# A twelve-layer decoder on one core: the logarithm of the state-space layer in parts between scans, and layer 2's causal mask added by TensorE

## The chip, the cores and the metric

One core of one Trainium2 chip runs the whole decoder in one launch. The metric is the device time of that launch in microseconds. The engines are named as in the profile: PE is TensorE (matmul; PEld are its weight loads), DVE is VectorE, ACT is ScalarE, POOL is GpSimd, SP is SyncE, which only issues DMAs here.

## The reference, cut to what matters

The input is four sequences of 512 tokens with 128 features, in fp32. Twelve sublayers run in turn, each followed by a residual sum and a layer normalization. Two of them are touched.

Layer 1's attention is a selective state-space layer: 256 inner channels with 16 states each.

```python
xc = silu(causal_conv(xi) + conv_b)
dt, Bm, Cm = split(xc @ W_x)
delta = softplus(dt @ W_dt + b_dt)
dA = exp(delta[..., None] * A);  dBu = delta[..., None] * Bm[:, :, None, :] * xc[..., None]
h = dA_t * h + dBu_t;  y = einsum('bdn,bn->bd', h, C_t)      # a scan over the 512 tokens
return (ys + xc * D) * silu(z) @ W_out
```

Layer 2's attention has 16 heads of width 64 and a causal mask.

```python
logits = jnp.einsum('bhik,bhjk->bhij', q, k)
logits = jnp.where(tril(ones((L, L))), logits, -1000000.0)
y = einsum('bhij,bhjv->bhiv', softmax(logits, axis=-1), kv)
```

## The kernel before

The order of instructions on every engine is the order in which the Python code issues them: the kernel switches the framework's own scheduling off, and the code interleaves by hand. A layer is a generator that issues a piece of work at each `yield`; heads and tails of neighbouring layers are interleaved, the bodies run alone. An `Agenda` maps a step number to pieces that are issued when `run(step)` is reached. The framework adds the semaphores that the data and the buffers need. Each engine takes its own queue in order, so a waiting instruction holds up all that stands behind it on its engine.

**The state-space layer** (`l1_attn`, from L1997) holds channels on partitions, in two halves c = 0 and 1 of 128, and time along the free axis. It goes through the four sequences; each has eight steps, and a step handles two of the 16 states. Below, "step 0" to "step 7" are the steps of one sequence (`j` in the code), and `g` counts them over all four. A step issues, in this order:
- `recurred(g)`: on DVE two products, du times the broadcast B (L2136, for c = 0 and 1), then two scans of 1024 elements (L2139); after each scan POOL multiplies the result h by C (L2143).
- `decays(g + 1)`: on ACT four exponentials da of the next step (L2125), two for each half of `de`.
- on PE `summed(g - 1, 0)` (L2152, adds h into the accumulator acc), then the pieces of the agenda `early`, then the broadcasts of B (pb, L2111) and C (pc, L2117) for the next step and half 0, then `summed(g - 1, 1)`, then pb and pc for half 1. ACT copies pc to cs (L2118).
- at step 0 the `outputs` of the sequence before: two DVE instructions on acc (L2161), a POOL product with the gate sz (L2164), and later a projection yps on PE (L2173, step 7), its sum with the residual (L2179), the statistics (L334, L335) and, at the next step 0, the normalization (L346) and the transposition.

While a sequence is scanned, the next one is prepared in pieces (`prepare`): the agenda `early` does the convolution of half 0 at step 1, of half 1 at step 2, `selected` (dt, B, C) at step 3, `exponentials(0)` at step 4 and `exponentials(1)` at step 5, and the gates (psz on PE, L2045, and Silu on ACT, L2046) at step 6. `exponentials(c)` makes on PE the tile pdt (L2065) and on ACT seven functions of it, three squares sq among them (L2076). The softplus needs a logarithm: `logarithm(c)` is a polynomial in five DVE instructions of 512 elements each (three at L2085, two at L2087), which work in place on the tile pdt. They are issued at the end of step 4 (half 0) and at the end of step 5 (half 1), after that step's scans. `ends` adds the result to `de` and makes `du` on POOL, two instructions of 1024 elements (L2090, L2091), at the head of step 6.

PSUM is tight here. pb tiles have two buffers, so the next step's pb of a half waits for this step's scan of that half. The tiles pscv, px, pdt, psz, yps and the transposes share a ring that has one bank, `a1`.

**Causal attention** (class `Causal`, L1112 to L1203) is used by layer 1's expert layer and by layer 2's attention (`l2_attn`, from L1453). A unit is a pair of heads of one sequence; layer 2 has 4 x 8 = 32 units. The query tiles of a unit are handled in three parts (`PARTS`): tile 3 with 512 keys; tiles 2 and 0 with 384 and 128; tile 1 with 256. For each part PE makes the scores of both heads (L1137), with one head in the upper and one in the lower 64 rows of the array. Then `maxima` on DVE does one `tensor_tensor_reduce` for each tile and head (L1153), eight in a unit: it adds the mask tile, negates, writes the result back to PSUM and reduces its minimum to nm. `exps` on ACT takes exp(-x + nm) and the sums zs (L1161), and `norm` divides on DVE (L1167) and POOL (L1170). `turned` transposes on PE (L1186), and `products` multiplies with v (L1199). The mask tile is bf16: 384 columns of zero and then 128 by 128 with -2^100 above the diagonal.

A step of layer 2 issues the scores of unit i + 1 and the rest of unit i; PE's order is: scores of part 0, the last product of the unit before, transposes of key part 0, queries and keys psqk of unit i + 2, scores of part 1, transposes, product 0, output projection ypo, scores of part 2, transposes psv of v, transposes, product 1. All these PSUM tiles take turns in a ring of three buffers, so each waits until the third one before it is read out. psv so waits for the exponentials of part 1.

Of the kernel before, what the change touches and what calls it, by code (L numbers as in the profile page):

```python
# [15 lines left out]
AF = mybir.ActivationFunctionType  # L16
ALU = mybir.AluOpType
AX = mybir.AxisListType
# [3 lines left out]
P = 128  # L22
B, S, D = 4, 512, 128
# [70 lines left out]
def _layer_params(name, p):  # L94
# [80 lines left out]
def decoder_kernel(ctx: ExitStack, tc: tile.TileContext, x, ctxT, mask1, mask3, packs, offsets, out, layers):  # L175
    nc = tc.nc
# [131 lines left out]
    identb = const.tile([P, P], BF16, name="identb")  # L308
# [803 lines left out]
    class Causal:  # L1112
# [4 lines left out]
        KEYS = (((0, 0),), ((1, 0), (3, 384)), ((2, 0),))  # L1117
        WIDTH = (512, 512, 256)

        def __init__(self, pool, room):  # L1120
            self.ap, self.room, self.work = pool, room, None

            self.mask = pool.tile([P, S], BF16, name="cmaskb", bufs=1)
            nc.gpsimd.memset(self.mask[:, : S - P], 0.0)
            make_causal_mask(nc, self.mask[:, S - P :], MASKED)
            self.nm = {}
            self.pr = {}
            self.pT = {}

        def scores(self, u, part, q, k):  # L1130

            sc = psum2("scc")
            for i, (qt, at) in enumerate(self.PARTS[part]):
                n = (qt + 1) * P
                for r in range(2):
                    rows = slice(64 * r, 64 * r + 64)
                    nc.tensor.matmul(  # L1137
                        sc[:, r, at : at + n], lhsT=q[rows, qt * P : n], rhs=k[rows, :n], start=(i == 0), stop=True,
                        skip_group_check=True,
                    )  # L1140
            nt = len(self.PARTS[part])
            nm = small.tile([P, 2, 2], F32, tag=f"nm{part}", name="nm")
            zs = small.tile([P, 2, 2], F32, tag=f"zs{part}", name="zs")
            pr = self.ap.tile([P, 2, self.WIDTH[part]], F32, tag=f"pr{part}", name="pr")
            self.pr[u, part] = pr

            def maxima():

                for i, (qt, at) in enumerate(self.PARTS[part]):
                    n = (qt + 1) * P  # L1150
                    for r in range(2):
                        of = sc[:, r, at : at + n]
                        nc.vector.tensor_tensor_reduce(  # L1153
                            of, of, self.mask[:, S - n :], -1.0, 3.0e38, ALU.add, ALU.min, nm[:, i, r : r + 1]
                        )

            def exps():
                for i, (qt, at) in enumerate(self.PARTS[part]):
                    to = at + (qt + 1) * P
                    for r in range(2):  # L1160
                        nc.scalar.activation(  # L1161
                            pr[:, r, at:to], sc[:, r, at:to], AF.Exp, bias=nm[:, i, r : r + 1], scale=-1.0,
                            accum_out=zs[:, i, r : r + 1],
                        )
# [40 lines left out]
    def l1_ffn(w, cur, new, last, room):  # L1205
        NH, NE, DH, NC = 8, 8, 64, 4
        units = B * NC
        keep, pool = room.take("keep"), room.take("early")
        causal = Causal(pool, room)
# [215 lines left out]
        first, then, last_of = gate(0)  # L1425
# [27 lines left out]
    def l2_attn(w, cur, new, last, room):  # L1453
        NC = 8
        units = B * NC
        keep, pool = room.take("keep"), room.take("early")
# [4 lines left out]
        causal = Causal(pool, room)  # L1461
        made, ypo, oTs = {}, {}, {}
        agenda = Agenda()
        state_x, state_T = cur["x"], cur["xT"]
# [532 lines left out]
    def l1_attn(w, cur, new, last, room):  # L1997
# [20 lines left out]

        das, work = [], []
        made = {}  # L2020
        early, late = Agenda(), Agenda()

        def prepare(b):

# [4 lines left out]
            ab = one.tile([P, 2, S], F32, tag="ab", name="ab")  # L2029
            ln = one.tile([P, 2, S], F32, tag="ln", name="ln")  # L2030
# [47 lines left out]
                    nc.scalar.activation(na, w["alog"], AF.Exp)  # L2078
                    nc.vector.tensor_scalar(na, na, -1.0, None, ALU.mult)

            def logarithm(c):

                e, sq = es.pop(c), squares.pop(c)
                for i, (_, _, number) in enumerate(LOG1P_T):
                    nc.vector.scalar_tensor_tensor(e, sq[:, i, :], number, e, ALU.add, ALU.mult)  # L2085
                for number, to in zip(LOG1P, (e, ln[:, c, :]), strict=True):
                    nc.vector.scalar_tensor_tensor(to, e, number, ab[:, c, :], ALU.add, ALU.mult)  # L2087
# [5 lines left out]
            return (  # L2093
                [
                    lambda: convolved(0), lambda: convolved(1), selected, lambda: exponentials(0),
                    lambda: exponentials(1), lambda: (gates(0), gates(1)),
                ],
                [lambda: logarithm(0), lambda: logarithm(1)],
                ends,
            )  # L2100

# [27 lines left out]
        def recurred(g):  # L2129

            b, j = divmod(g, steps)
            m = made[b]
            m["h", j] = [work[0].tile([P, NQ, S], F32, tag=f"hh{c}", name=f"hh{c}") for c in range(2)]
            pbs = [m.pop(("B", j, c)) for c in range(2)]
            for c in range(2):
                nc.vector.tensor_tensor(pbs[c], m["du"][:, c, None, :].to_broadcast([P, NQ, S]), pbs[c], ALU.mult)  # L2136
            for c in range(2):
                flat = m["h", j][c].rearrange("p n t -> p (n t)")
                nc.vector.tensor_tensor_scan(  # L2139
                    flat, das[g % 2][:, c].rearrange("p n t -> p (n t)"), pbs[c].rearrange("p n t -> p (n t)"),  # L2140
                    0.0, ALU.mult, ALU.add,
                )
# [51 lines left out]
        for i in (0, 1, 5, 2, 3, 4):  # L2194
            first[i]()
            yield PIECE
            if i in (3, 4):
                second[i - 3]()
# [15 lines left out]
        for g in range(total + 1):  # L2214
            b, j = divmod(g, steps)
            if j == 1 and b + 1 < B:
                first, second, third = prepare(b + 1)
                early.add(g, first)
                late.add(g + 3, second)
            if j == 6 and b + 1 < B:  # L2220
                third()
            if g < total:
                recurred(g)
            if g + 1 < total:
# [187 lines left out]
```

## Time and profile before

| what | value |
|---|---|
| runs | 2703.14 us median of 3 (2700.03 to 2704.36) |
| profiled execution | 2705.39 us; its span 2703.4 us, granted clock 0.963 |
| PE | 2410.7 us busy, 89% of the span |
| DVE | 1754.2 us, 65% |
| ACT | 1247.0 us, 46% |
| POOL | 1056.1 us, 39% |
| the state-space layer's steps | about 547 to 823 us |
| layer 2's causal attention | about 1437 to 1850 us |
| L2139, the 64 scans | 142.6 us, 2270 ns each |
| L1153, the 384 masked maxima (192 of them in the other layer) | 191.5 us, 499 ns each |
| L1137, scores | 142.5 us |

A profile line of a group names line, engine, operation, out<-in with partitions x elements and type, and a count; fp32 matmuls appear as two records each. A timeline line gives the start and the duration in us and merges neighbours of the same kind. In brackets stands the idle time of that engine just before, and the instruction whose end released it.

### The profile page before, as it was taken

The numbers are of one execution on the slowest core, as the hardware profiler recorded it, in microseconds if no ns is written. First come the engines' busy times: TensorE is split into PE (matmuls) and PEld (weight loads), VectorE is DVE, ScalarE is ACT, GpSimd is POOL, SyncE is SP. The second block draws the span as 40 slices with busy tenths as digits, with TensorE's granted clock in tenths as the row PEclk, the third lists the DMA queues.
The fourth block names the chain that finished last, engine by engine and source line by source line (L and its number), as shares of the span: only waits on it lengthen the run. The fifth ranks groups of instructions, "written<-read, shape, count | busy, mean of one in ns | idle before, by whom it ended". The sixth has DMA issues, their size and how long they took to land.

```text
span 2703.4 us, 37772 instructions
## 1 busy us (share of the span) xinstructions
PE 2410.7 (89%) x13974; PEld 1161.6 (43%) x13994; DVE 1754.2 (65%) x3484; ACT 1247.0 (46%) x2525; POOL 1056.1 (39%) x1376
## 2 busy tenths in 40 slices
PE   5898889978877989999999999997988999999998
PEld 1233334433334434444444555554455233446665
DVE  6796951288896665555556666666756887664444
ACT  3676432377652434333333455453543787443221
POOL 2342520166675336556542444443445343310000
PEclk9998999989998999999999999998998999999999
DMA  5421310000002400000000000002102241400000
GB/s 152 119 79 57 101 35 0 0 0 0 0 16 80 142 7 1 0 1 1 1 1 1 15 12 1 13 13 83 39 1 59 77 115 23 139 24 1 4 5 8
DMA packets 75560, 96.39 MB, mean 36 GB/s; under 512 B 23664, under 2 KB 62320, under 8 KB 75376
## 3 DMA queue, kind: packets, MB, share of 16 engines
q1 hardware_dynamic: 74224, 92.14, 11.7%
q8 instruction: 110, 1.80, 0.3%
q10 hardware_dynamic: 1152, 1.84, 0.2%
q14 instruction: 74, 0.61, 0.1%
HBM read 63.92 MB, written 33.49 MB: 36 GB/s over the span
## 4 chain that ended last, share of the span: by engine, by line
PE 62%; DVE 16%; ACT 9%; POOL 5%; issue 4%; DMA 2%; SPq 1%; POOLq 0%; DVEq 0%; ACTq 0%
PE psgu L1935 4%; PE psve L1289 4%; PE av L709 4%; PE yT L1332 3%; PE scc L1137 3%; PE ype L1946 3%; ACT pr L1161 3%; PE psh L1624 3%; DVE scc L1153 3%; PE avc L1199 3%; PE ptc L1186 3%; DVE top L967 2%; PE sc L670 2%; PE avx L995 2%; DVE top L674 2%
## 5 line engine op out<-in xcount | busy, mean ns | idle before, releaser
L1170 POOL TENSOR_TENSOR pr<-pr,zs 128x1024 f32<-128x1024 f32 x192 | 237.4, 1254 | 246.6 <-DVE zs L1167 232.4
L674 DVE TENSOR_REDUCE top<-sc 128x2 f32<-128x1024 f32 x256 | 300.8, 1216 | 46.8 <-PE sc L670 43.0
L695 ACT ACTIVATE pT<-st 128x512 f32<-128x512 f32 x512 | 276.1, 597 | 89.0 <-PE st L686 85.8
L1161 ACT ACTIVATE pr<-scc,nm 128x256 f32<-128x256 f32 (+3 forms) x384 | 199.0, 530 | 198.2 <-DVE zs L1167 78.3
L1153 DVE CUSTOM_DVE_ANT_0 scc<-scc,cmaskb 128x256 f32<-128x256 f32 (+3 forms) x384 | 191.5, 499 | 131.4 <-PE scc L1137 112.6
L967 DVE TENSOR_REDUCE top<-scx 128x4 f32<-128x616 f32 x256 | 192.1, 794 | 88.1 <-PE scx L954 77.2
L973 ACT ACTIVATE pTx<-stx 128x512 f32<-128x512 f32 x256 | 139.3, 596 | 202.8 <-PE scx L954 135.5
L2143 POOL TENSOR_TENSOR hh<-hh,cs 128x1024 f32<-128x1024 f32 x64 | 149.4, 2355 | 74.0 <-DVE hh L2139 50.1
L709 PE MATMUL av<-pT,vbuf 128*32 128x256 f32 x2048 | 162.8, 393 | 8.4 <-ACT avs L509 8.4
L492 POOL CAST nmP<-top 128x16 bf16<-128x16 f32 x96 | 25.6, 267 | 363.7 <-DVE top L967 202.5
L1294 DVE TENSOR_TENSOR vtmp<-psve,gm 128x1024 f32<-128x1024 f32 x64 | 78.3, 1224 | 133.2 <-PE psve L1289 133.1
L337 POOL TENSOR_TENSOR rsf<-mvf,eps 128x4 f32<-128x4 f32 x48 | 9.9, 206 | 393.7 <-DVE mvf L335 392.6
L1137 PE MATMUL scc<-k,q 64*128 64x512 f32 (+3 forms) x768 | 142.5, 469 | 10.8 <-ACT pr L1161 6.2
L1186 PE MATMUL ptc<-ident,pr 128*128 128x128 f32 x960 | 138.4, 282 | 10.3 <-ACT pT L1533 5.7
L2139 DVE TENSOR_TENSOR_SCAN hh<-da,pb 128x1024 f32<-128x1024 f32 x64 | 142.6, 2270 | 0.0
L1289 PE MATMUL psve<-w_L_ffn,xT 128*128 128x512 f32 x256 | 125.7, 615 | 17.4 <-ACT pr L1161 11.9
L670 PE MATMUL sc<-kP,qP 64*128 64x512 bf16 x512 | 106.3, 414 | 35.1 <-DMA qP<-far_q 16.6
L1299 POOL TENSOR_TENSOR vtmp<-vtmp 128x512 f32<-128x512 f32 x60 | 76.0, 1267 | 153.9 <-DVE vtmp L1294 133.6
L2152 PE MATMUL acc<-hh,ident 128*128 128x512 f32 x256 | 132.5, 644 | 3.1 <-DVE yt L2161 1.9
L1199 PE MATMUL avc<-pT,v 128*64 128x512 f32 (+3 forms) x768 | 131.2, 449 | 0.8 <-DVE pT L1522 0.5
L1186 PEld LDWEIGHTS ptc<-ident,pr 128*128 128x128 f32 x960 | 103.4, 141 | 55.1 <-issue 13.9
L1332 PE MATMUL yT<-gT,w_L_ffn 128*128 128x512 f32 x256 | 122.9, 603 | 0.0
(418 smaller groups left out, 5044.4 us busy)
## 6 DMA issues: line engine op xcount, KB each, us to landing
qP<-far_q SPq DMA_DIRECT2D x24, 768.0 KB, 6.3
w_L_ffn<-in_L_ffn SPq DMA_DIRECT2D x24, 512.0 KB, 6.5
far_q<-part SPq DMA_DIRECT2D x44, 192.0 KB, 2.8
qP<-far_q SPq DMA_DIRECT2D x24, 256.0 KB, 4.1
far_q<-part SPq DMA_DIRECT2D x44, 128.0 KB, 2.4
kP<-far_k SPq DMA_DIRECT2D x7, 768.0 KB, 5.3
kP<-far_kc SPq DMA_DIRECT2D x16, 231.0 KB, 4.5
w_L_attn<-in_L_attn SPq DMA_DIRECT2D x6, 512.0 KB, 6.6
```

The source lines that it names most:

```text
L674: return lambda: nc.vector.tensor_reduce(top[:, qt, 2 * gp : 2 * gp + 2], sc, AX.X, ALU.max, negate=True)
L695: nc.scalar.activation(pT, st, AF.Exp)
L709: nc.tensor.matmul(m["av"][32 * g : 32 * g + 32, part], lhsT=m["v"][:, kt, 4 * j + g, :], rhs=weights_of[s, g][:, part], start=(kt == 0 an ...
L967: nc.vector.tensor_reduce(ops.maxima(a)[:, 2 * qp : 2 * qp + 2, 2 * gp : 2 * gp + 2].rearrange("p i r -> p r i"), sc, AX.X, ALU.max, negat ...
L1137: nc.tensor.matmul(sc[:, r, at : at + n], lhsT=q[rows, qt * P : n], rhs=k[rows, :n], start=(i == 0), stop=True, skip_group_check=True,)
L1153: nc.vector.tensor_tensor_reduce(of, of, self.mask[:, S - n :], -1.0, 3.0e38, ALU.add, ALU.min, nm[:, i, r : r + 1])
L1161: nc.scalar.activation(pr[:, r, at:to], sc[:, r, at:to], AF.Exp, bias=nm[:, i, r : r + 1], scale=-1.0, accum_out=zs[:, i, r : r + 1],)
L1170: nc.gpsimd.tensor_tensor(pr[:, :, at : at + n], pr[:, :, at : at + n], zs[:, i, :, None].to_broadcast([P, 2, n]), ALU.mult)
L1186: nc.tensor.transpose(pt[:, r, to : to + P], self.pr[u, p][:, r, lo : lo + P], ident)
L1199: nc.tensor.matmul(av[64 * r : 64 * r + 64, kt * P :], lhsT=v[:, kt, 64 * r : 64 * r + 64], rhs=self.pT[u, part][:, r, at : at + n], start ...
L1289: nc.tensor.matmul(ps[:, r, :], lhsT=src[:, t * P : (t + 1) * P], rhs=w["ve"][:, h * 512 : (h + 1) * 512], start=True, stop=True,)
L1332: nc.tensor.matmul(yTs[b], lhsT=oe[:, c, e, :], rhs=gT[:, i, :], start=(c == 0 and e == 0), stop=(c == NC - 1 and e == NE - 1),)
```

## The change

In the state-space layer:
- The five instructions of each half's logarithm are split three and two. Half 0: three at the end of step 4 as before, two in step 5, between the two scans. Half 1: three between the scans of step 6, two between the scans of step 7.
- The sums `ends` work on one half at a time, with 512 elements: half 0 between the scans of step 6, half 1 between the scans of step 7, on POOL behind h of half 0.
- The gates move from step 6 to step 0 of the sequence itself.
- Before the first sequence the logarithms stay whole; the sums come in halves.

In layer 2's attention alone (`by_pe`):
- PE adds the mask: for each tile and head one more product, identity (bf16, weights) times the 128 by 128 mask, accumulated onto the last 128 columns of the scores; eight in a unit, 256 in all, each with its own weight load.
- DVE takes the negated maximum of the scores with one plain `tensor_reduce` for each tile and both heads, four in a unit, and doesn't write the scores back.
- The exponentials take scale 1 for -1.

```diff
-                        sc[:, r, at : at + n], lhsT=q[rows, qt * P : n], rhs=k[rows, :n], start=(i == 0), stop=True,
+                        sc[:, r, at : at + n], lhsT=q[rows, qt * P : n], rhs=k[rows, :n], start=(i == 0), stop=not self.by_pe,
...
+            if self.by_pe:
+                for qt, at in self.PARTS[part]:
+                    for r in range(2):
+                        nc.tensor.matmul(
+                            sc[:, r, at + qt * P : at + (qt + 1) * P], lhsT=identb, rhs=self.mask[:, S - P :],
+                            start=False, stop=True, skip_group_check=True,
+                        )
...
+                    if self.by_pe:
+                        nc.vector.tensor_reduce(nm[:, i, :], sc[:, :, at : at + n], AX.X, ALU.max, negate=True)
+                        continue
...
-            def logarithm(c):
-
-                e, sq = es.pop(c), squares.pop(c)
-                for i, (_, _, number) in enumerate(LOG1P_T):
-                    nc.vector.scalar_tensor_tensor(e, sq[:, i, :], number, e, ALU.add, ALU.mult)
-                for number, to in zip(LOG1P, (e, ln[:, c, :]), strict=True):
-                    nc.vector.scalar_tensor_tensor(to, e, number, ab[:, c, :], ALU.add, ALU.mult)
-
-            def ends():
-                nc.gpsimd.tensor_tensor(m["de"], m["de"], ln, ALU.add)
-                nc.gpsimd.tensor_tensor(m["du"], m["de"], m["xc"], ALU.mult)
+            def logarithm(c, ops=range(5)):
+
+                e = es[c]
+                for i in ops:
+                    if i < len(LOG1P_T):
+                        nc.vector.scalar_tensor_tensor(e, squares[c][:, i, :], LOG1P_T[i][2], e, ALU.add, ALU.mult)
+                    else:
+                        to = ln[:, c, :] if i == len(LOG1P_T) + 1 else e
+                        nc.vector.scalar_tensor_tensor(to, e, LOG1P[i - len(LOG1P_T)], ab[:, c, :], ALU.add, ALU.mult)
+
+            def ends(c):
+                nc.gpsimd.tensor_tensor(m["de"][:, c, :], m["de"][:, c, :], ln[:, c, :], ALU.add)
+                nc.gpsimd.tensor_tensor(m["du"][:, c, :], m["de"][:, c, :], m["xc"][:, c, :], ALU.mult)
...
                 nc.gpsimd.tensor_tensor(m["h", j][c], m["h", j][c], m["C", j], ALU.mult)
+                if c == 0 and g in between:
+                    between.pop(g)()
...
                 first, second, third = prepare(b + 1)
-                early.add(g, first)
-                late.add(g + 3, second)
-            if j == 6 and b + 1 < B:
-                third()
+                early.add(g, first[:5])
+                early.add(g + 7, first[5:])
+                late.add(g + 3, [lambda f=second: f(0, range(3))])
+                between[g + 4] = lambda f=second: f(0, range(3, 5))
+                between[g + 5] = lambda f=second, h=third: (h(0), f(1, range(3)))
+                between[g + 6] = lambda f=second, h=third: (f(1, range(3, 5)), h(1))
```

More of the change, by code (lines that the diff above doesn't have):

```diff
@@ L1118, in decoder_kernel, with __init__ @@
         WIDTH = (512, 512, 256)
-        def __init__(self, pool, room):
-            self.ap, self.room, self.work = pool, room, None
+        def __init__(self, pool, room, by_pe):
+            self.ap, self.room, self.work, self.by_pe = pool, room, None, by_pe
             self.mask = pool.tile([P, S], BF16, name="cmaskb", bufs=1)
@@ L1161, in exps @@
                         nc.scalar.activation(
-                            pr[:, r, at:to], sc[:, r, at:to], AF.Exp, bias=nm[:, i, r : r + 1], scale=-1.0,
+                            pr[:, r, at:to], sc[:, r, at:to], AF.Exp, bias=nm[:, i, r : r + 1],
+                            scale=1.0 if self.by_pe else -1.0,
                             accum_out=zs[:, i, r : r + 1],
@@ L1208, in l1_ffn @@
         keep, pool = room.take("keep"), room.take("early")
-        causal = Causal(pool, room)
+        causal = Causal(pool, room, False)
         made, gates, yTs, oTs, gTs, waiting = {}, {}, {}, {}, {}, []
@@ L1460, in l2_attn @@
         wo = w["wo"].rearrange("p (c d) -> p c d", c=NC)
-        causal = Causal(pool, room)
+        causal = Causal(pool, room, True)
         made, ypo, oTs = {}, {}, {}
@@ L2020, in l1_attn @@
         made = {}
-        early, late = Agenda(), Agenda()
+        early, late, between = Agenda(), Agenda(), {}
         def prepare(b):
@@ L2097, in prepare @@
                 ],
-                [lambda: logarithm(0), lambda: logarithm(1)],
+                logarithm,
                 ends,
@@ L2197, in l1_attn @@
             if i in (3, 4):
-                second[i - 3]()
+                second(i - 3)
                 if i == 3:
                     yield PIECE
-        third()
+        for c in range(2):
+            third(c)
         yield PIECE
@@ L2217, in l1_attn @@
                 first, second, third = prepare(b + 1)
-                early.add(g, first)
-                late.add(g + 3, second)
-            if j == 6 and b + 1 < B:
-                third()
+                early.add(g, first[:5])
[4 more added lines that the diff above has]
+                between[g + 6] = lambda f=second, h=third: (f(1, range(3, 5)), h(1))
             if g < total:
```

## The prediction

> **What bounds the kernel now.** Page first: PE is busy for 89% of the span, but the change touches two stages with different limits, so I read each alone, in the busy times by stretch. In 548 to 823 us (the state-space layer) DVE is busy 253.90 of 275 us and PE 217.29; in 1437 to 1841 us (layer 2's causal attention) PE is busy 372.46 of 404 us, DVE 271.64. So the first stage is DVE's and the second PE's. Next I read the timelines for what is left over. First layer 2, one unit (one head pair) of PE and then of DVE; columns are start us, duration us, engine, line, and in brackets the idle time before and who ended it:
>
> ```profile
> 1754.19 1.13 PE L1137 MATMUL scc<-k,q 64*128 64x512 f32 x4
> ...
> 1758.57 1.14 PE L1137 MATMUL scc<-k,q 64*128 64x384 f32 x8
> 1759.64 1.09 PE L1186 MATMUL ptc<-ident,pr 128*128 128x128 f32 x8
> ...
> 1762.76 0.70 PE L1137 MATMUL scc<-k,q 64*128 64x256 f32 x4
> 1764.01 0.66 PE L1481 MATMUL psv<-ident,k 128*128 128x128 f32 x4 [0.55 <-ACT pr L1161]
> 1764.91 0.66 PE L1186 MATMUL ptc<-ident,pr 128*128 128x128 f32 x4 [0.25 <-ACT pT L1533]
> 1765.50 1.08 PE L1199 MATMUL avc<-pT,v 128*64 128x384 f32 x8
> 1766.51 1.13 PE L1137 MATMUL scc<-k,q 64*128 64x512 f32 x4
> ```
>
> ```profile
> 1759.86 0.56 DVE L1153 CUSTOM_DVE_ANT_0 scc<-scc,cmaskb 128x384 f32<-128x384 f32 x1 [0.43 <-PE scc L1137]
> ...
> 1761.79 0.14 DVE L1153 DVE_READ_ACCUMULATOR2_ANT nm<- 128x1 f32 x1
> ```
>
> A unit takes 1766.51 - 1754.19 = 12.32 us, of which PE idles 0.55 + 0.25 = 0.80. It idles for exp on ACT, which waits for DVE's four masked maxima of part 1 (1759.86 to 1761.93, 2.07 us). Now the state-space layer, DVE and then PE, steps 4 to 7 of its second sequence (a step starts with the two products of L2136):
>
> ```profile
> 657.37 2.16 DVE L2085 SCALAR_TENSOR_TENSOR pdt<-sq,pdt 128x512 f32<-128x512 f32 x3 [2.43 <-ACT sq L2076]
> ...
> 660.90 2.35 DVE L2136 TENSOR_TENSOR pb<-du,pb 128x1024 f32<-128x1024 f32 x2
> 663.16 4.46 DVE L2139 TENSOR_TENSOR_SCAN hh<-da,pb 128x1024 f32<-128x1024 f32 x2
> ...
> 678.05 1.23 DVE L2136 TENSOR_TENSOR pb<-du,pb 128x1024 f32<-128x1024 f32 x1 [0.30 <-PE psz L2045]
> 681.65 1.23 DVE L2136 TENSOR_TENSOR pb<-du,pb 128x1024 f32<-128x1024 f32 x1 [2.37 <-PE pb L2111]
> ```
>
> ```profile
> 661.03 1.12 PE L2065 MATMUL pdt<-rest,w_L_attn 8*128 8x512 f32 x2 [1.08 <-DVE ln L2087]
> 665.49 1.04 PE L2111 MATMUL pb<-bc,pick 128*128 128x512 bf16 x2 [3.34 <-DVE hh L2139]
> 666.32 0.63 PE L2117 MATMUL pc<-bc,pick 128*128 128x512 bf16 x1
> 666.75 3.57 PE L2152 MATMUL acc<-hh,ident 128*128 128x512 f32 x4
> 670.15 0.60 PE L2111 MATMUL pb<-bc,pick 128*128 128x512 bf16 x2
> 670.59 0.38 PE L2117 MATMUL pc<-bc,pick 128*128 128x512 bf16 x1
> 670.80 1.88 PE L2152 MATMUL acc<-hh,ident 128*128 128x512 f32 x4
> ```
>
> DVE is dense but for some 20 us of stalls in all. The gates (psz, step 6) make the broadcast pb late in step 7: 0.30 + 2.37 us. The same L2152 group of four takes 3.57 us after PE has idled 3.34 us, and 1.88 us a moment later: an idle PE comes back at half clock. The granted clock of 657 to 671 us is 0.76.
>
> **Layer 2's masks.** Per unit DVE loses eight masked maxima and their eight accumulator reads and gets four plain reductions. A reduction of 128x1024 from PSUM takes 1216 ns (L674) and one of 616 takes 794 (L967): 1.03 ns an element over about 155, so 768 and 256 take 0.95 and 0.42. Part 1 falls from 2.07 to about 1.30, -0.77 us. PE gets eight bf16 products of 128x128 with their weight loads. Nearest row: L503, the same shape with a load each, eight from 210.33 to the next instruction's 210.89: 0.56 us, 70 ns each. Bounds: 55 ns (pb, two of 512 bf16 columns in 0.44 us, a quarter each) and 136 ns (ypo L1492, eight fp32 records from 1761.67 to 1762.76). I take 70, as it has type, shape and loads in common.
>
> Behind part 1's scores the chain becomes 0.77 - 0.28 (four masks) = 0.49 shorter, and two more masks lie in front of PE's wait: both idle times go. What is late next is PE itself: 12.32 - 0.80 + 0.56 = 12.08, -0.24 a unit (-0.13 for units that idled 0.69). Not all units gain. In each later sequence of eight, the unit with the normalization (13.5 us, idle 1.35, mostly behind L346 on DVE) gives -0.79; the next, which sends queries (idle 0.57), 0; the one after waits for POOL (0.74 + 0.34), whose work hangs on PE's ps_proj, and gives +0.05; five regular ones -0.98. Together -1.7, three times: -5.2. In the first sequence the units that send keys (12.65, idle 1.01) keep some 0.4 of it: about -1.0; the end of the stage -0.4. **Sum -6.6 us.** At 55 ns it is about -10.5, at 136 ns about +10.
>
> [...]
>
> **The state-space layer.** Logs: the same 10 instructions a sequence (0.69 to 0.72 us); three of the first half stay at the end of step 4, so the 2.43 us wait for ACT's squares stays. The halves on POOL are two times some 1.16 us (L412, 512 columns) for each 2.35: the same sum, POOL is 69% busy. At the head du may come up to 0.5 us sooner, which I leave out. Table loads for Silu stay as many.
> - Gates leave step 6: the stalls 0.30 + 2.44, 0.30 + 2.37 and 0.46 + 1.14 go: **-7.0**.
> - Step 5 to 6. The first half's tile pdt sits in the only PSUM bank of its ring (a1), so PE's pdt of the second half waits until the last two logs end, now 1.4 us behind step 5's first scan. Queued on PE behind it: pb and pc of step 6, acc, the second pb. From that log's end: pdt 1.72 at half clock (0.86 a record), pb 0.85, pc 0.43, one acc record 0.86 and three at 0.43, pb 0.45, some 5.7 us. DVE in the same time has a scan and one product, 2.25 + 1.2 = 3.45. So DVE stalls about **2.3**, three times: +6.9. Before, the five logs at the end of step 5 (3.5 us) covered just this. At full clock the stall is 0.35; at half clock throughout, 3.9.
> - Step 7. The projection yps of the sequence before takes a1 too, and now waits for the second half's last logs; PE idles some 3.6 us and its 16 records run 3.5 us, not 1.95: ys is late by 1.5 (0 at full clock), in the two sequences that have it: +3.0.
> - Step 0, the gates' new place. ACT must first do decays, whose second half waits for POOL's de (released a log later than the scan), then copies, then a table load: silu ends about 7.1 us into the step, the second gate 8.0, pb and pc 8.65, acc 10.4. The output's second L2161 would start at 7.5 in the first sequence: +2.9 (to 4.5 at half clock). Later ones have 3.3 us of normalization in front (L346) and are covered, but for 0.6 at a copy of xT.
>
> **Sum** -7.0 + 6.9 + 3.0 + 3.5 = **+6.4**; with a fully clocked PE -7.0 + 1.1 + 2.9 + 0.6 = -2.4; with a half-clocked one -7.0 + 11.7 + 3.0 + 6.5 = +14.
>
> [...]
>
> Total -6.6 + 6.4 = -0.2 us. The profiled execution took 2705.39 us, its span 2703.4 and 2.0 around it; it stands 2.25 above the median of the runs, 2703.14. Taken from the median: **2703 us**, no change.
>
> **Rivals.**
> - Faster: PE keeps its clock over the new waits. [...] Then -2.4 with layer 2 between -6.6 and -10.5: -9 to -13, about 2692.
> - Slower, by the one bank a1: pdt and yps wait inside steps and come back at half clock for whole groups, as the 3.57 us row shows. +14 - 6.6 = +7.4, about 2711; it decides from 1.8 us of stall over my figure a sequence.
> - Slower by the masks: weight loads and the change between row-tiled fp32 and bf16 make a mask cost 136 ns. +10 + 6.4: about 2719. Against: L503's 70 ns, between fp32 neighbours.
> - That the logs don't get between the scans is excluded: in DVE's order of the built program they stand there.
>
> **Numbers.** 0.2% (5.4 us) is about what a measurement of this kernel can tell from no change. Forecast 0.38; faster 0.33; slower by a1 0.22, by masks 0.07. So faster 0.33, same 0.38, slower 0.29. Cases of both signs weigh as much as the middle, so the range reaches to both: 2690 to 2716; the forecast's own is 2698 to 2708.
>
> **What would show it.** L1137's neighbours: eight bf16 records a unit, 0.56 us together; DVE's part 1 near 1.3 us; units of 12.1 us without the 0.55 and 0.25. In the state-space layer: no psz stall in step 7; idle before the second L2136 product of step 6 near 1.9 us, released by pb; idle before ys in step 7; before the second L2161 of the first sequence about 3 us. Wrong if the granted clock stays near 1 there, if a mask costs far from 70 ns, or if PE idles elsewhere in layer 2.

## The result and the profile after

The changed kernel takes 2703.51 us, median of 12 runs (2699.47 to 2706.66); beside it the kernel before took 2701.74 us, median of 12 (2694.77 to 2705.08). The ratio is 1.0008, with an interval of 0.9999 to 1.0017, which is +2.2 us (-0.3 to +4.6): no change that this measurement can tell. Behind that stand two changes of some 10 us each, of opposite sign.

The profiled execution took 2701.54 us, its span 2699.3 us. Spans of two executions can't be compared to the microsecond: the same code in front of the state-space layer ends at 546.17 us in the kernel before and at 542.73 us in another execution of it (the run `masks_only` below). So I compare stages. The state-space stage is measured from DVE's residual sum just ahead of it (546.17 us before, 543.41 after) to the start of the last sequence's normalization (L346; 826.95 and 836.78): 280.78 us before, **293.37 after, +12.6**. Layer 2 is measured from the start of its second unit to the start of its last: 381.31 before, **371.31 after, -10.0**. The sum, +2.6, agrees with the +2.2 of the runs.

Busy times by stretch of the changed kernel (PE, PEld, DVE, ACT, POOL with counts, then the granted clock):

```profile
548.00:823.00 275.00, 210.07 (x541) 89.15 (x550) 240.64 (x198) 173.19 (x269) 182.10 (x103) 0.91 0.02 4
1437.00:1841.00 404.00, 394.67 (x2440) 218.31 (x2439) 234.23 (x414) 204.06 (x609) 178.21 (x164) 1.00 0.04 9
```

DVE, which sets the first stretch, is busy for 240.64 us where it was 253.90: it waits more. PE, which sets the second, is at 394.67 of 404 with a clock of 1.00, as before: 9.3 us of this stretch are left without PE work, where it was 31.5. One unit of layer 2 in PE's timeline of the changed kernel, with the new products at L1144:

```profile
1754.35 1.13 PE L1137 MATMUL scc<-k,q 64*128 64x512 f32 x4
1755.41 0.29 PE L1144 MATMUL scc<-cmaskb,identb 128*128 128x128 bf16 x2
...
1760.02 0.40 PE L1144 MATMUL scc<-cmaskb,identb 128*128 128x128 bf16 x4
1760.25 1.04 PE L1197 MATMUL ptc<-ident,pr 128*128 128x128 f32 x8
...
1763.96 0.28 PE L1144 MATMUL scc<-cmaskb,identb 128*128 128x128 bf16 x2
1764.08 0.61 PE L1492 MATMUL psv<-ident,k 128*128 128x128 f32 x4
1764.75 0.66 PE L1197 MATMUL ptc<-ident,pr 128*128 128x128 f32 x4
...
1766.35 1.13 PE L1137 MATMUL scc<-k,q 64*128 64x512 f32 x4
```

The unit takes 12.00 us. There is no bracket in front of psv and ptc any more: PE's two waits are gone. Four masks push the transposes from 1760.02 to 1760.25, 58 ns each. On DVE the maxima of part 1 are now two reductions:

```profile
1760.45 1.29 DVE L1159 TENSOR_REDUCE nm<-scc 128x2 f32<-128x768 f32 x2 [0.65 <-PE scc L1144]
```

In the state-space layer, DVE's stalls of the second sequence and, first line, at the start of it:

```profile
627.14 0.75 DVE L2176 SCALAR_TENSOR_TENSOR yt<-xc,w_L_attn,acc 128x512 f32<-128x512 f32 x1 [3.21 <-PE acc L2167]
...
669.57 1.23 DVE L2149 TENSOR_TENSOR pb<-du,pb 128x1024 f32<-128x1024 f32 x1 [0.94 <-PE pb L2124]
674.26 1.23 DVE L2149 TENSOR_TENSOR pb<-du,pb 128x1024 f32<-128x1024 f32 x1 [3.46 <-PE pb L2124]
...
681.84 2.33 DVE L2149 TENSOR_TENSOR pb<-du,pb 128x1024 f32<-128x1024 f32 x2
...
691.45 0.69 DVE L2194 TENSOR_TENSOR ys<-yps,x 128x512 f32<-128x512 f32 x1 [1.58 <-PE yps L2188]
```

The two products of step 7 (681.84) have no bracket; step 6, ys and the output of step 0 have new ones. The chain of work through step 6 says why (start us, duration us, what):

```profile
665.75 0.70 DVE ln L2100
666.45 0.04 issue
666.50 2.07 PE pdt L2076 x2
668.57 0.97 PE pb L2124 x2
669.53 0.43 PE pc L2130
669.96 3.41 PE acc L2167 x4
673.37 0.87 PE pb L2124 x2
```

The last logarithm of half 0 frees the bank a1, and from there to the end of the second pb PE needs 7.8 us, all of it at the durations of a half clock: acc 3.41 us for four records, where four take 1.88 at full clock. In front of pdt PE had idled 5.39 us. The same wait of 5.39 us stands at this place in all three sequences that prepare a next one; from pdt's start the granted clock is 0.50 for 5.0, 7.6 and 5.7 us, and the stalls before the two products of step 6 grow with it: 0.94 + 2.17, 0.94 + 3.46 and 0.93 + 2.54 us.

### The profile page after: what moved, and what is told of

Its sections match the earlier page's. It is cut to its first block, busy times and chain, and to the rows that moved or that the text cites. A ratio compares the mean times of both kernels' runs of the same rounds, so it can differ in the third digit from the quotient of the medians.

```text
span 2699.3 us, 37935 instructions
## 1 busy us (share of the span) xinstructions
PE 2422.1 (90%) x14230; PEld 1174.1 (43%) x14250; DVE 1713.8 (63%) x3100; ACT 1248.9 (46%) x2525; POOL 1058.1 (39%) x1384
## 4 chain that ended last, share of the span: by engine, by line
PE 64%; DVE 15%; ACT 8%; POOL 5%; issue 4%; DMA 3%; SPq 1%; POOLq 0%; DVEq 0%; ACTq 0%
PE psgu L1946 4%; PE av L709 4%; PE psve L1300 4%; PE scc L1137 4%; PE yT L1343 3%; PE avc L1210 3%; PE ype L1957 3%; PE ptc L1197 3%; PE psh L1635 3%; ACT pr L1171 2%; PE sc L670 2%; DVE top L967 2%; PE psqk L1482 2%; PE avx L995 2%; PE st L686 2%
## 5 line engine op out<-in xcount | busy, mean ns | idle before, releaser
L1159 DVE TENSOR_REDUCE nm<-scc 128x2 f32<-128x1024 f32 (+3 forms) x128 | 102.4, 821 | 119.8 <-PE scc L1144 119.8
```

## The experiments

Each run's ratio is to the kernel before on the same chip. The medians come from several chips, so runs are better compared by their ratios. The last column is the state-space stage as measured above, from one execution each. It shifts too: the changed kernel and logs_only have the same code there and differ by 2.4 us, mostly in a stall at step 0 that ends with PE's acc (3.21 and 4.84 us).

| run | median us | ratio (interval) | state-space stage us |
|---|---|---|---|
| changed kernel | 2703.51 | 1.0008 (0.9999 to 1.0017) | 293.37 |
| masks_only | 2690.93 | 0.9958 (0.9946 to 0.9970) | 280.69 |
| logs_only | 2715.12 | 1.0045 (1.0029 to 1.0060) | 295.80 |
| log_in_sbuf | 2715.64 | 1.0045 (1.0032 to 1.0059) | 301.54 |
| masks_gates0 | 2689.42 | 0.9946 (0.9934 to 0.9959) | 277.05 |
| keep_clock | 2687.02 | 0.9938 (0.9926 to 0.9950) | 281.29 |
| half0_whole | 2699.23 | 0.9983 (0.9973 to 0.9993) | 287.97 |
| masks_twice | 2701.35 | 0.9988 (0.9978 to 0.9997) | 281.23 |
| gates_apart | 2701.87 | 0.9993 (0.9983 to 1.0003) | 285.65 |
| logs_later | 2694.89 | 0.9975 (0.9966 to 0.9984) | 286.53 |
| logs_later_gates | 2692.22 | 0.9963 (0.9949 to 0.9978) | 286.13 |
| masks_both | 2696.73 | 0.9984 (0.9974 to 0.9994) | 277.05 |
| logs_later_2 | 2683.08 | 0.9927 (0.9912 to 0.9943) | 272.29 |

**My theory** was that the bank a1 makes PE wait in steps 5 and 7, and that PE's half clock behind these waits is what DVE then stalls for. **Rivals**: the logarithms at the end of step 5 were needed as cover whatever the bank does; the gates are the cost; the masks gain nothing by themselves.

### The two parts alone

masks_only is the kernel before with `by_pe` in layer 2 and nothing changed in `l1_attn`:

```diff
-        causal = Causal(pool, room)
+        causal = Causal(pool, room, True)
```

> The kernel before with layer 2's masks on PE alone, the state-space layer untouched. Theory (two effects that cancel): the change's masks shorten layer 2, whose 29 units between the second and the last take 381.3 us before and 371.3 after in the traces, so this runs about 10 us below the kernel before, some 0.37%, with units of 12.00 us. Rival (neither part does anything, and the stage lengths of single executions shift about): within 3 us of the kernel before.

logs_only is the changed kernel with the state-space part alone:

```diff
-        causal = Causal(pool, room, True)
+        causal = Causal(pool, room)
```

> The changed state-space layer alone, layer 2 as before. Theory: the steps from the last sum of the layer in front to the last normalization take 280.8 us before and 293.4 after, so this runs about 12 us above the kernel before, 0.45%, with DVE idle of 3 to 4.4 us in step 6 of each of three sequences, 1.6 at ys in step 7 and 3.2 at step 0. Rival: within 3 us of the kernel before.

Measured: -11.4 us (-8.1 to -14.6) and +12.2 us (+7.8 to +16.2). They add up to +0.8, against +2.2 for both together, which the intervals can't tell apart. So the even result is a gain and a loss that cancel; that one part changes what the other does is not seen, though an effect of a few us could hide in these intervals.

### What a mask costs

masks_twice issues each mask's product twice:

```diff
                 for r in range(2):
-                    nc.tensor.matmul(
+                    for i in range(2):
+                        nc.tensor.matmul(
```

> The kernel before with layer 2's masks on PE, each mask product issued twice (the values of masked logits double, which changes nothing behind the softmax). Against masks on PE alone, 2690.9: theory, layer 2 is now bound by PE all through, so 256 more products cost their own time: at the 58 ns that four in a row took 15 us (unit 12.00 to 12.46, 2706), at 70 ns 18 us (2709). Rival: part of them runs in waits of PE that the trace shows as work, under 8 us, below 2699.

Units went from 12.00 to 12.33 or 12.34 us, the stretch from unit 2 to the last from 371.53 to 381.31. That is 0.335 us for eight more masks, 42 ns each: 9.8 us over the units, between the two expectations. The PE rows of masks_twice:

```profile
1761.14 0.62 PE L1145 MATMUL scc<-cmaskb,identb 128*128 128x128 bf16 x8
1761.60 1.04 PE L1198 MATMUL ptc<-ident,pr 128*128 128x128 f32 x8
...
1765.54 0.61 PE L1493 MATMUL psv<-ident,k 128*128 128x128 f32 x4
1766.09 0.66 PE L1198 MATMUL ptc<-ident,pr 128*128 128x128 f32 x4
```

The eight take 0.46 us, again 58 ns each, so as a part of PE's stream a mask costs 58 ns. But psv to ptc is 0.55 us here and was 0.67 in the changed kernel (1764.08 to 1764.75): it seems that a wait of some 0.12 us was left inside psv's row, with no bracket to show it, and that the further masks took it up; that is the 0.13 us between 0.46 and 0.335. A similar price shows in masks_both, which sets `by_pe` in layer 1's expert layer too (on masks_gates0):

```diff
-        causal = Causal(pool, room, False)
+        causal = Causal(pool, room, True)
```

> The kernel with both gates inside step 0, whole logarithms and layer 2's masks on PE (2689.4), with the masks on PE in layer 1's expert layer too, which uses the same class. Theory: there PE has the products of the expert layer between the parts and idles less for the exponentials, so the 256 masks' 58 ns each stand mostly on PE's path: 5 to 12 us slower than 2689. Rival: DVE's maxima set that stage too, and it gains as layer 2 did: 5 to 10 us faster.

The expert layer has 16 units and so 128 masks, not the 256 that I wrote there (and the 192 maxima that the table of the time before gives to that layer are 128 in the trace). From its second unit to the first of layer 2 it took 428.51 us against 420.88: +7.6 us, 64 ns for each of the 120 masks of these 15 units. PE's wait for the exponentials stayed as it was in most units, here in masks_gates0 and then in masks_both:

```profile
1257.06 1.98 PE L1300 MATMUL psve<-w_L_ffn,xT 128*128 128x512 f32 x4 [1.27 <-ACT pr L1171]
```

```profile
1264.11 1.98 PE L1300 MATMUL psve<-w_L_ffn,xT 128*128 128x512 f32 x4 [1.27 <-ACT pr L1171]
```

So the masks paid in layer 2, where both waits of PE went, and not in the expert layer, where they stayed; why the shorter work on DVE doesn't shorten the wait there is open. That the change leaves the expert layer alone is worth those 7.6 us.

### The bank a1, first try

log_in_sbuf lets the logarithm work in SBUF, so that a1 is free as soon as ACT has read it (one ACT function less, too):

```diff
-                e = es[c]
+                e = ln[:, c, :]
...
-                nc.scalar.activation(pd, ab[:, c, :], AF.Exp, scale=-1.0)
```

> The changed kernel, but the logarithm works in place in SBUF (in ln, its first factor read from ab, which holds the same exponential), so that the PSUM bank a1 is free once ACT has read pdt; the copy of the exponential that ACT wrote to pdt is left out, eight ACT instructions of 0.6 us. Theory: the stalls of steps 6 and 7 come from the bank: PE's 5.4 us and 3.2 us waits for the last log go, the 3.1 to 4.4 us of DVE idle in step 6 fall below 1 and the 1.6 at ys to 0; the stall at step 0 stays near 3. So 11 to 15 us below the changed kernel. Rival (the logs between the scans cost by themselves, as they push the second scan and POOL back): the stalls stay, and it runs at most 2 us below the changed kernel.

It was 10 us slower than the changed kernel by the ratios, 8.2 in the stage. The stalls did go: no bracket before step 6's products and none before ys, and pdt ran at 664.72 without a wait. The loss is elsewhere. Three rows of log_in_sbuf on DVE, the first in the head where POOL has nothing to do, and one on POOL:

```profile
531.17 0.69 DVE L2096 SCALAR_TENSOR_TENSOR ln<-sq,ab 128x512 f32<-128x512 f32 x1
...
660.99 2.15 DVE L2096 SCALAR_TENSOR_TENSOR ln<-sq,ab 128x512 f32<-128x512 f32 x1 [0.67 <-ACT sq L2086]
663.25 3.45 DVE L2096 SCALAR_TENSOR_TENSOR ln<-sq,ln 128x512 f32<-128x512 f32 x2
```

```profile
660.23 5.11 POOL L2154 TENSOR_TENSOR hh<-hh,cs 128x1024 f32<-128x1024 f32 x2
```

With both operands in SBUF the same instruction takes 0.69 us while POOL is idle and 2.15 beside POOL's product; POOL's two take 5.11, where two take 4.66 in the changed kernel. From 545 to 840 us the 30 logarithm instructions cost 51.6 us against 20.5 with one operand in PSUM: 31 us more on the engine that sets the stage. With pdt in PSUM three of these instructions took 2.15 us in the changed kernel (658.52, beside POOL's two of 4.66 us from 656.00). As a test of the theory the run decides little: the bank was free, but the slower logarithms between the scans (3.42 us for two at 671.07, where two take 1.4) give PE cover as well, so the stalls may have gone for either reason.

### The clock

keep_clock keeps the order of the changed kernel and fills PE's two new waits with products that add zero:

```diff
+        zero = row32[:, 0:1]
+        nc.vector.memset(zero, 0.0)
+        def kept_busy(b, n):
+            if b in made and "acc" in made[b]:
+                for _ in range(n):
+                    nc.tensor.matmul(made[b]["acc"][0], lhsT=zero.to_broadcast([P, P]), rhs=state_T[:, b, :], ...)
...
+                if c == 1:
+                    kept_busy(b - 1, 6)
                 pd = es[c] = psum_a("pdt")
...
+                kept_busy(b + 1, 4)
                 yp = psum_a("yps")
```

> The changed kernel, with products that add zero (a zero column as weights, the transposed state as moving data, accumulated onto acc) in PE's two new waits: six, some 5.2 us, ahead of pdt of half 1 in step 5, four, some 3.5 us, ahead of yps in step 7. They leave out nothing. Theory: the waits for the bank a1 hurt through the clock that PE comes back with; kept busy, PE runs pdt, pb, pc and acc at full clock, so the stalls before the second product of step 6 (3.1, 4.4, 3.5 us in the changed kernel) fall to 0.4 to 1.2 and those before ys (1.6, 1.7) to under 0.5: together 9 to 12 us less, about 2693. Rival: the stalls are the wait itself and the order of PE's queue, whatever the clock: stalls as they are, time 2703 or, with the products running over, up to 2710.

It is 19 us faster than the changed kernel by the ratios; the stage is 12.1 us shorter, the profiled span 13.5. What the runs gain beyond that is open. PE in keep_clock, the same place as the chain above, and DVE's two products behind it:

```profile
659.59 5.83 PE L2035 MATMUL acc<-xT,row 128*128 128x512 f32 x12
665.35 1.12 PE L2087 MATMUL pdt<-rest,w_L_attn 8*128 8x512 f32 x2
666.40 0.61 PE L2135 MATMUL pb<-bc,pick 128*128 128x512 bf16 x2
666.84 0.38 PE L2141 MATMUL pc<-bc,pick 128*128 128x512 bf16 x1
667.06 1.88 PE L2178 MATMUL acc<-hh,ident 128*128 128x512 f32 x4
668.77 0.59 PE L2135 MATMUL pb<-bc,pick 128*128 128x512 bf16 x2
```

```profile
667.04 1.23 DVE L2160 TENSOR_TENSOR pb<-du,pb 128x1024 f32<-128x1024 f32 x1 [0.95 <-PE pb L2135]
669.41 1.23 DVE L2160 TENSOR_TENSOR pb<-du,pb 128x1024 f32<-128x1024 f32 x1 [1.14 <-PE pb L2135]
```

From pdt to the second pb it is 3.42 us (665.35 to 668.77), where it was 6.66 in the changed kernel (666.50 to 673.16). The granted clock from 548 to 823 us is 0.97 for 0.91. Step 6's stalls are 0.80, 0.95 + 1.14 and 0.80, together 3.7 us for 11.0; those before ys in the second and third sequence are gone (one of 1.42 us comes at the last sequence's end, where nothing is filled). The wait for the bank is still there: PE spends it on zeros. So most of the loss, some 12 us, is the clock behind the wait, and the rival that the clock doesn't matter falls. The wait itself is not free: in the first and third sequence 0.80 us of stall is left, ended by pb; in the second the zeros ran 1.45 us past the bank's release (663.90). With whole logarithms and the gates moved (masks_gates0 below) step 6 has no stall, and the stage is 4.2 us shorter still.

### The bank or the lost cover

half0_whole puts half 0's logarithm back to the end of step 4, whole, so that pdt of half 1 finds the bank free:

```diff
-                late.add(g + 3, [lambda f=second: f(0, range(3))])
-                between[g + 4] = lambda f=second: f(0, range(3, 5))
+                late.add(g + 3, [lambda f=second: f(0)])
```

> The changed kernel, with half 0's logarithm whole at the end of step 4 as it was before; half 1's stays split, so the bank a1 is free when PE reaches pdt of half 1 in step 5, but the end of step 5 still has no logarithm that covers PE. Theory of two parts: the wait for a1 goes, the lost cover stays: stalls before the second product of step 6 near 1.9 us each (pb at half clock behind the scan) for 3.1 to 4.4, ys unchanged at 1.6: 4 to 6 us less than the changed kernel, about 2698.5. Rival a, only the wait for a1 counts: stalls under 0.5, 11 us less, 2692.5. Rival b, only the lost cover counts: stalls as they are, 2703.

Measured 6.8 us below the changed kernel by the ratios, 5.4 in the stage; stalls in step 6 of 2.23, 1.43 and 2.52, and ys late by 1.68 and 1.40, much as in the changed kernel. The theory of two parts holds. PE in half0_whole:

```profile
664.71 2.07 PE L2076 MATMUL pdt<-rest,w_L_attn 8*128 8x512 f32 x2
669.15 1.03 PE L2124 MATMUL pb<-bc,pick 128*128 128x512 bf16 x2 [2.37 <-DVE hh L2152]
669.98 0.63 PE L2130 MATMUL pc<-bc,pick 128*128 128x512 bf16 x1
670.40 2.95 PE L2167 MATMUL acc<-hh,ident 128*128 128x512 f32 x4
673.19 0.59 PE L2124 MATMUL pb<-bc,pick 128*128 128x512 bf16 x2
```

PE now waits for the scan instead, comes back slow all the same (acc 2.95 us for 1.88), and nothing at the end of step 5 covers it. The kernel before had this slow group too (acc 3.57 us) and no stall in step 6; there five logarithms stood at the end of step 5.

### The gates

masks_gates0 takes from the change only the masks and the gates' new place; logarithms and sums stay whole where they were:

```diff
-                early.add(g, first)
+                early.add(g, first[:5])
+                early.add(g + 7, first[5:])
```

> The masks on PE, and of the state-space edits the gates' move to step 0 alone; logarithms whole at the ends of steps 4 and 5, sums whole at the head of step 6. Theory: the split of the logarithm costs (it holds the bank a1 into the next steps), the gates' move gains: step 7's stalls (7.0 us in all) go, step 0 of the first sequence gets 1 to 3 us, the xT copy 0.6 to 1.5. So 3 to 5 us below masks_only, 13 to 15 below the kernel before. Rival (the gates cost as much at step 0 as at step 6): like masks_only, 10 below.

The stage is 3.6 us shorter than in masks_only (277.05 for 280.69), and the other runs with the same code there agree (277.05 in masks_both, 280.78 before, 281.23 in masks_twice): the gates' move by itself is a gain. In the times it is 1.5 us by the medians and 3.2 by the ratios, too little to resolve. What the gates still cost stands in masks_gates0's PE and DVE rows of step 0:

```profile
616.01 1.02 PE L2056 MATMUL psz<-xT,w_L_attn 128*128 128x512 f32 x2
619.49 1.71 PE L2056 MATMUL psz<-xT,w_L_attn 128*128 128x512 f32 x2 [2.46 <-ACT sz L2057]
```

```profile
624.71 0.75 DVE L2172 SCALAR_TENSOR_TENSOR yt<-xc,w_L_attn,acc 128x512 f32<-128x512 f32 x1 [4.07 <-PE acc L2163]
```

The second gate waits for the first one's Silu, as both use a1. gates_apart puts one at the end of step 6 and one at the end of step 0:

```diff
-                early.add(g + 7, first[5:])
+                behind.add(g + 5, first[5:6])
+                behind.add(g + 7, first[6:])
...
+            behind.run(g)
```

> Masks on PE, logarithms whole at their old places, and the gates one at a time behind the broadcasts of a step instead of in front of them: half 0's at the end of step 6, half 1's at the end of step 0. Against the kernel with both gates inside step 0 (2689.4): theory, a gate delays DVE only by what stands behind it on PE, so the stalls of that kernel before the output's second instruction (4.1 us in the first sequence, 1.5 in the second) go, and no new one comes as a step leaves PE some 1.5 us: 4 to 6 us less, about 2684.5. Rival: PE is late into the next step (acc, pb) by the gate's 0.85 to 1.7 us, and DVE stalls before a product there by as much: within 2 us of 2689.

It was some 13 us slower than masks_gates0, against theory and rival. The 4.07 us did go, but DVE got stalls elsewhere: 1.34 to 1.46 us before the second product of step 7 in each sequence, 1.12 us in the second step behind a gate, 2.83 us (for 0.42) before a copy of xT; the stage grew by 8.6 us. The edit also cut the head into one more piece: the stage starts at 550.63 us, 7 us later, and its first scan comes another 2.5 us later than in masks_gates0; so the run changes more than the gates. From 562 to 822 us ACT does 24 table loads of 1.28 us where it did 17, as the two gates no longer share one. Which of these counts most is not told apart.

### A better order

logs_later puts each logarithm whole between the scans of the step behind its squares; nothing of a1 is then late for yps, and DVE doesn't wait 2.4 us for the squares, as it does in the kernels above (0.67 in log_in_sbuf):

```diff
-                late.add(g + 3, [lambda f=second: f(0, range(3))])
-                between[g + 4] = lambda f=second: f(0, range(3, 5))
-                between[g + 5] = lambda f=second, h=third: (h(0), f(1, range(3)))
-                between[g + 6] = lambda f=second, h=third: (f(1, range(3, 5)), h(1))
+                between[g + 4] = lambda f=second: f(0)
+                between[g + 5] = lambda f=second, h=third: (h(0), f(1), h(1))
...
+                if c == 1:
+                    kept_busy(b - 1, 8)
```

> The changed kernel with each half's logarithm whole between the two scans of the step behind its squares (half 0 in step 5, half 1 in step 6), the sums of both halves in step 6, and eight products that add zero ahead of pdt of half 1 in step 5, none ahead of yps (a1 is free again before step 7). Theory: the 2.4 us in which DVE waits for the squares in every kernel so far go, three times, as the squares come before the scan ends; the wait for a1 in step 5 is longer by three logs, but the products keep PE's clock, so the second product of step 6 waits no more than about 1 us; the waits before ys go. Against the changed kernel with products (2687.0): 6 to 9 us less, about 2680. Rival: the longer wait makes pdt, and with it ACT's seven functions and its copies cs, so late that POOL and PE hold up DVE in step 6 or 7 by as much: 2687 or more.

The squares' wait was gone, but the eight products of zero were too many. PE in logs_later, then DVE:

```profile
657.64 2.82 PE L2035 MATMUL acc<-xT,row 128*128 128x512 f32 x6
```

```profile
659.05 2.28 DVE L2163 TENSOR_TENSOR_SCAN hh<-da,pb 128x1024 f32<-128x1024 f32 x1
666.38 1.23 DVE L2160 TENSOR_TENSOR pb<-du,pb 128x1024 f32<-128x1024 f32 x1 [5.06 <-PE pb L2135]
```

PE came to them at 657.64 and the bank was free at 659.05; the products ran until 664.69 and made pdt late by 5.6 us. Eight such products take 7.0 us; the wait was 1.4 here and in the third sequence, 3.2 in the first. logs_later_gates adds two such products between the gates:

```diff
             def gates(c):
+                if c == 1:
+                    kept_busy(b - 1, 2, 1)
```

> The same, with two more products that add zero between the gates in step 0, where PE waits 2.5 us for Silu and then runs at half clock. Theory: the second gate, pb, pc and acc run at full clock, and the 3.2 us stall before the output's second instruction in the first sequence falls by 1.5 to 2.5 us, those of later sequences by less: 2 to 3 us less than the run beside it. Rival: the stall is the wait for Silu itself: within 1 us.

The stall before the output's second instruction stayed (2.38 for 2.37 us) and the stage is the same within 0.4 us, which speaks for the rival: there the wait for Silu itself counts. The time is 2.7 us lower by the medians, as the theory had it, but the intervals of the two ratios overlap, and the rows show no place for it. The last run has two products in place of eight:

```diff
-                    kept_busy(b - 1, 8)
+                    kept_busy(b - 1, 2)
```

> The logarithms whole between the scans of steps 5 and 6, as in the run with eight products that add zero, but with two of them. There PE had nothing to do from 657.64 and the bank a1 came free at 659.05 (second sequence), so that six of the eight ran past it: DVE waited 5.06 us before the first product of step 6 (3.22, 5.06, 5.05). Theory: two products (1.76 us) end as the bank comes free, pdt and pb run at full clock, those three stalls go and the 1.14 us before the second product stay: 11 to 13 us less than 2694.9, about 2682.5, and 4 us less than the changed kernel with products in its waits (2687.0), since the waits for the squares are gone. Rival: with PE idle or just busy pdt comes no sooner for DVE, as ACT (seven functions of pdt, then the copies cs, behind which pc and acc wait 2.1 us on PE) is the chain in steps 5 and 6: stalls of 3 us or more stay, 2688 or more.

Measured 2683.08 us, ratio 0.9927, 13 us less than logs_later by the ratios. PE and DVE in logs_later_2:

```profile
653.68 1.02 PE L2035 MATMUL acc<-xT,row 128*128 128x512 f32 x2
654.63 1.12 PE L2087 MATMUL pdt<-rest,w_L_attn 8*128 8x512 f32 x2
655.69 0.60 PE L2135 MATMUL pb<-bc,pick 128*128 128x512 bf16 x2
656.13 0.38 PE L2141 MATMUL pc<-bc,pick 128*128 128x512 bf16 x1
656.35 1.88 PE L2178 MATMUL acc<-hh,ident 128*128 128x512 f32 x4
```

```profile
656.33 1.23 DVE L2160 TENSOR_TENSOR pb<-du,pb 128x1024 f32<-128x1024 f32 x1
658.70 1.23 DVE L2160 TENSOR_TENSOR pb<-du,pb 128x1024 f32<-128x1024 f32 x1 [1.14 <-PE pb L2135]
```

In this sequence step 6's first product has no stall and the second waits 1.14 us. In the first the stall is 0.80; in the third 0.15 + 2.19, both ended by PE's pb; why pb came later there is open. The stage takes 272.29 us, 21.1 less than in the changed kernel and 8.5 less than before; of the 8.5 some 3.6 are the gates' move, and against masks_gates0 4.8 are left (the two ratios' intervals overlap). So the change's idea, logarithms between the scans, is worth some 5 us when the bank comes free as PE gets to it. Without the two products I didn't run it.

## Why the prediction was right, and where it was not

The time was predicted at 2703.0 and came out at 2703.51. The mechanisms were the right ones, but the two stages were mis-sized by some 3 and 6 us of opposite sign, which nearly cancelled: that the time came within 0.5 us is luck.

- **Layer 2, -6.6 predicted, -10.0 in the trace** (-11.4 by the runs of masks_only). Both idle times went and PE became the bound, as the step says. The mis-sized term is the price of a mask: 70 ns taken from L503, 58 ns measured (its lower end was 55); by the step's own ends, -6.6 at 70 ns and -10.5 at 55, 58 ns gives -9.7. Then 12.32 - 0.80 + 0.46 = 11.98, and the unit takes 12.00 where the step had 12.08. Part 1's two reductions take 1.29 us (1.30 predicted). The units with extra work gained 0.59, 0.12 and 0.34 where I had 0.79, 0 and a loss of 0.05: the third idled the 0.55 and 0.25 too, and 13.85 - 0.80 + 0.46 = 13.51 is what it takes. The first sequence's units gained 2.5 where I had 1.0.
- **Gates leave step 6, -7.0.** Right: no stall is left before the products of step 7.
- **Step 5 to 6, +2.3 a sequence predicted, 3.1, 4.4 and 3.5 measured** (0.94 + 2.17, 0.94 + 3.46, 0.93 + 2.54): +11.0 for +6.9. The queue behind pdt was read rightly; the failed step is the line "one acc record 0.86 and three at 0.43". The step let the clock return 3.9 us after pdt's start (1.72 + 0.85 + 0.43 + 0.86), an estimate that no run shows; it came back after 5.0, 7.6 and 5.7 us, in the second sequence behind the whole group and the second pb. The end that the step gave for that, 3.9 a sequence, is near the mean of what came (3.7). keep_clock shows that the clock is the cause of most of it; with PE kept busy there 0.80 us is left in the first and third sequence, where the step had 0.35 at full clock.
- **yps in step 7, 1.5 twice.** 1.58 and 1.68 measured; its 16 records took 3.68 us for the 3.5 predicted.
- **Gates at step 0, +2.9 and 0.6 predicted.** In the first sequence 3.21. The copy of xT waits 2.52 for 1.14, +1.4 where I had 0.6, and 1.06 for 0.64 at the head, where unchanged code took 0.60 to 0.88 in other runs; waits of 0.47 for du and 0.43 for pb at step 0 were not foreseen.
- **Sum of the state-space layer, +6.4 predicted, +12.6 in the trace**: close to the term with a half-clocked PE, +14. So in this layer the rival "slower, by the one bank a1" came true, and the masks gave back what its total lacked. The rival with masks at 136 ns fell, and so did the one in which PE keeps its clock, until keep_clock made it so.

## What to carry to other kernels

A wait on PE can cost more than its length when what stands behind it is on another engine's path: look at the durations of the group after the wait. Here, after 5.39 us, 5.0 to 7.6 us of work ran at half clock, so the safe sum takes the whole group at half clock. Before splitting a piece of work that works in place on a PSUM bank, list who needs that bank next and when PE gets there; here logarithms between the scans gained only in the one run where the bank came free about as PE got to it. And when a change has two parts in stages with different limits, measure them apart: here -11 and +12 us looked like nothing.

## What the runs showed of the hardware that I had not expected

- The logarithm's DVE instruction with two SBUF operands took 0.69 us with POOL idle and up to 2.72 us beside POOL's products; 30 of them cost 31 us more than with one operand in PSUM.
- After 5.39 us without work PE ran at half clock for 5.0, 7.6 and 5.7 us in the three sequences. Shorter waits differ: after 2.46 us in masks_gates0 (619.49) the half clock lasted until about 623 us (acc from 622.27 took 2.40 us, where 1.88 is full clock), and after 2.46 us at the same place in the changed kernel (623.62) PE ran at full clock (granted 1.00 from 623.60 to 628.00).
- A 128-column bf16 product with its own weight load is a row of 219 ns, but four or eight in a stream cost 58 ns each; the start of the next instruction gives the price, not the row's own duration.
